# A two-layer graph network on one core: first weight chunks loaded and flipped by half columns, neighbour sums issued singly behind half products

## The chip, the cores and the metric

The kernel runs on one core of a Trainium2 chip. That core has a matrix engine (TensorE, "PE" in the profile), a vector engine (VectorE, "DVE"), a scalar engine (ScalarE, "ACT"), a general-purpose engine (GpSimd, "POOL") that here issues the indexed transfers, and SyncE ("SP"), which issues the plain ones. Each engine works through its own queue of instructions; a scheduler fixes the order of each queue when the kernel is built, and semaphores make one engine wait for another. The metric is the device time of one launch in microseconds (us), lower is better.

## What is computed

`x` has 2708 rows of 1024 numbers in fp32, and `adj` is a 0/1 matrix of 2708 x 2708 with few ones (the first rows have the most). The reference is

```python
# layer 0: attention over the neighbours of each row
q, k, v = x @ Wq.T + bq, x @ Wk.T + bk, x @ Wv.T + bv
z = (q @ k.T) / sqrt(1024) * adj
z = where(z == 0, -10000, z)
x = layernorm(x + relu(softmax(z, axis=1) @ v))
# layer 1: sum over the neighbours of each row
x = layernorm(x + adj @ (x @ W1) + b1)
```

Since `adj` is sparse, the kernel never forms the 2708 x 2708 scores. It reads `adj` once, makes of each row a list of its neighbours' numbers, and gathers the neighbours' rows. The scores come from one product `y = x M`, with M made of Wq and Wk ahead of everything else, and layer 1 is worked out as `(adj @ x) @ W1`. A dense version of the whole lies behind a test of the data and isn't executed here.

## The kernel before

**Tiles.** The rows are worked on in 22 blocks of 128 (block numbers 0 to 21). `SLOTS` says for each block how many neighbours its longest list has: 15 for block 0 down to 0 for blocks 20 and 21. Rows with very long lists, the hub, are dealt out over a block of parts of their own (`"hub"`, `HUB_SLOTS = 11`), whose partial sums in `part` are brought back by a matmul with the 0/1 matrices `to_h` and `to_0`.

**Products.** A product of two blocks with a 1024 x 1024 weight is made with seven half products instead of eight (`pair_products`, L335; `half_products`, L308): the weight's quarters w11, w12, w21, w22 are taken with three differences t2, t3, t4 (and t1, which overwrites w12), and the left side with four sums `s_all` of the turned blocks (L1212 to L1215). A half product is four matmuls of 128 x 128 by 128 x 512, which the profile shows as eight records at L311. Its result in PSUM is evicted by `add` (L333) or, in layer 1, by `whole` (L1517), both on DVE, with a priority that the scheduler puts ahead of other work. A block is turned ("flipped") by TensorE through PSUM, with ACT's copies of the result to SBUF: `flip` (L953, L954) takes one transpose for each 128 x 128 chunk, and `flip_shares` (L966) a matmul with a given matrix in place of the identity.

**The start.** SP's queue issues the loads in program order: the 8 chunks of WqT, then the 8 of WkT, each 512 KB (L142, L144), then pieces of `adj`. TensorE flips each chunk in two groups of four transposes as it lands (`flip_w`, L281), into one of three PSUM buffers (`p_tr`); the groups are copied out by ACT (L286) and DVE (L284) in turn. Meanwhile DVE forms Wq^T bk, one column of numbers from each chunk of Wq (`junkd`, L298), and POOL and ACT form Wk^T bq (L301, L302). The product of the two flipped weights, M, is the first work of `pair_products`, with its differences of weights made by DVE at L783 and L784.

**Between the layers.** When a block of layer 0 is done, it is normalised (`norm`, L998 to L1014; for the last block `norm_halves`, L1019 to L1032, on statistics by half rows at L1239) and scattered to `x_d` in device memory (L940, on POOL). Every gather of layer 1 reads `x_d`, so the first of them comes behind the last scatter. To keep TensorE busy across that, `WARM = 13` matmuls without use are put there (L1530). W1 is loaded by quarters at the end of layer 0 (L1447).

**Layer 1.** The blocks are worked on in ten units of two, in the order of `units` (L1456). For each block `sum_rows` (L1472 to L1484) issues one gather for each slot (`gather_slot`, L483, on POOL) into one of nine `g` tiles or, for slot 0 of an ordinary block, straight into the sum's tile `r`; then DVE adds it, with the slot's column of 0/1 flags in `valid` as a factor (L1480). Where slot 0 can be missing (blocks 0, 7, 18 and 19 and the hub), a pass of `tensor_scalar` masks it into `r` (L1477). Blocks 18 and 19 (`single`) have no other slot. `turn1` flips the sums of a unit; `gather_x1` (L467, L1490) gathers the block's own row onto a copy of the bias; `work1` makes the seven half products; `finish1` normalises and scatters to the output.

**What sets the order.** The instructions of one unit are written in the order finish of the unit before, flips of the unit after, sums of the third unit after, products (L1542 to L1563), and the hub's sums stand in unit 4. The sums of a block are written in one go, without a tie to TensorE except in unit 0, where `follow` ties the first of them behind the flipping of a unit. `between` is a table by which layer 0 hangs a function behind the half product of a given number; `half_products` calls it with its last matmul. In layer 1 of the kernel before it isn't used. The four differences of W1 (t1 to t4, L1537 to L1540) are written behind the first flips, and `follow(..., firsts[0], same=True)` holds t1 behind the first mask pass on DVE.

Of the kernel before, what the change touches and what calls it, by code (L numbers as in the profile page):

```python
# [9 lines left out]
F32 = mybir.dt.float32  # L10
# [11 lines left out]
P = 128  # L22
# [8 lines left out]
WARM = 13  # L31
# [53 lines left out]
def sparse_part(ctx, tc, x, xT, adj, wqT, wkT, wvT, bq, bk, bv, w1, b1, out):  # L85
# [28 lines left out]
    with es:  # L114
# [26 lines left out]
        for c in range(DC):  # L141
            nc.sync.dma_start(out=wq_i[c // 2][:, c % 2, :], in_=wqT[c * P:(c + 1) * P, :])  # L142
        for c in range(DC):
            nc.sync.dma_start(out=wk_i[:, c, :], in_=wkT[c * P:(c + 1) * P, :])  # L144
# [128 lines left out]
        def flip_w(dst, src):  # L273

            n = 0
            for c in range(DC):
                for g in range(DC // 4):
                    tr = p_tr.tile([P, 4, P], F32, name="tr")
                    for k in range(4):
                        o = g * 4 + k  # L280
                        put = nc.tensor.transpose(tr[:, k, :], src(c)[:, o * P:(o + 1) * P], ident)  # L281
                    to = dst(c, g)
                    if n % 2:
                        nc.vector.tensor_copy(to, tr)  # L284
                    else:
                        nc.scalar.copy(to, tr)  # L286
                    n += 1
            return put

# [3 lines left out]
        flip_w(lambda c, g: wq_of(c)[:, g * 4:g * 4 + 4, :], lambda c: wq_i[c // 2][:, c % 2, :])  # L293
        flipped = flip_w(lambda c, g: wk_o[g][c // 4][:, :, c % 4 * P:(c % 4 + 1) * P], lambda c: wk_i[:, c, :])
# [5 lines left out]
        for c in (*range(2, DC), 0, 1):  # L300
            nc.gpsimd.tensor_tensor(wk_i[:, c, :], wk_i[:, c, :], bq_bc, op=ALU.mult)  # L301
            put = nc.scalar.activation(junk[:, :D], wk_i[:, c, :], AF.Copy, accum_out=y_col[:, c:c + 1])  # L302
            follow(put, flipped)
# [1159 lines left out]
        firsts = []  # L1463

        def sum_rows(b, k=0, behind=None):
            if b == "hub":
                n, tab, ok, r = P, tab_h, valid_h, part
            else:
                n, tab, ok = (P, tab0, valid0) if b == 0 else (rows[b], tabs[:, b, :SLOTS[b]], valid[:, b, :SLOTS[b]])
                r = (cp if k else rp).tile([P, D], F32, name="r", bufs=3 if k else RB)  # L1470
            for j in range(tab.shape[1] if b else J0):
                if j == 0 and b not in [0, "hub"] + single + MIXED:  # L1472
                    gather_slot(x1_d[:, :], tab[:n, 0:1], n, r)
                    continue
                xg = gather_slot(x1_d[:, :], tab[:n, j:j + 1], n, g_tile())
                if j == 0:
                    put = nc.vector.tensor_scalar(r[:n], xg[:n], ok[:n, 0:1], None, op0=ALU.mult)  # L1477
                    firsts.append(put)
                else:
                    put = nc.vector.scalar_tensor_tensor(r[:n], xg[:n], ok[:n, j:j + 1], r[:n], op0=ALU.mult, op1=ALU.add)  # L1480
                if behind is not None:
                    follow(put, behind, same=True)
                    behind = None
            return r  # L1484
# [399 lines left out]
```

## Time and profile before

| | us |
|---|---|
| median of 3 runs | 1009.27 |
| lowest, highest | 1007.11, 1018.39 |
| profiled execution, its own time | 1011.19 |
| its span, first to last instruction | 1009.5 |
| TensorE busy, layer 1 from 725 to 996 us of the span | 257.7 of 271.0 |
| DVE busy, the same stretch | 186.6 |
| POOL busy, the same stretch | 178.2 |
| DVE busy, 30 to 60 us | 30.0 of 30.0 |

The profile's times count from the start of the span. L and a number is the line of the kernel. A line of a timeline gives the start, the duration of the instruction (or of a run of like ones, then with x and their number), the engine, line and operation, what it writes and reads, and in brackets the engine's idle time before it and what ended that. A line of the list of waits gives the waiting engine and line, what it waited for, then the total in us, the number of times and the longest. TensorE's granted clock averaged 0.983 of full speed over the span.

### The profile page before, as it was taken

How to read it: one execution, taken by the hardware profiler on the slowest of the kernel's cores; microseconds unless marked ns; L12 is line 12 of the kernel's file. 1: busy time of each engine (PE TensorE's matmuls, PEld its weight loads, DVE VectorE, ACT ScalarE, POOL GpSimd, SP SyncE). 2: the span in 40 equal slices, each digit the busy share in tenths (PEclk: the TensorE clock that was granted, in tenths of full speed). 3: DMA queues.
4: the chain of work that ended last, by engine and by line, in shares of the span. 5: the costliest groups of instructions: out<-in, count | busy, mean ns of one | idle time of the engine just before them, and what ended most of it. 6: DMA issues, size and time to landing. Idle time of an engine off the chain costs nothing.

```text
span 1009.5 us, 10470 instructions
## 1 busy us (share of the span) xinstructions
PE 957.8 (95%) x2723; PEld 452.3 (45%) x2723; DVE 815.7 (81%) x1813; ACT 461.5 (46%) x1142; POOL 553.2 (55%) x443
## 2 busy tenths in 40 slices
PE   7989999999999999999899999999899899999994
PEld 6434444444444444454444444444444444435441
DVE  8999996995678896998899999984668977868532
ACT  4553466655543434233643544563242444252832
POOL 3841056133677574445466785621877878868420
PEclk9999999999999999999999999999999999989998
DMA  8475687769889676346537897756887699977631
GB/s 346 152 238 177 209 262 223 232 229 249 237 250 326 219 231 211 118 141 194 167 97 227 266 304 236 220 170 228 199 285 226 210 319 338 300 234 199 213 105 45
DMA packets 101342, 222.92 MB, mean 221 GB/s; under 512 B 19492, under 2 KB 46892, under 8 KB 101272
## 3 DMA queue, kind: packets, MB, share of 16 engines
q0 software_dynamic: 49424, 152.74, 49.8%
q1 hardware_dynamic: 51848, 69.41, 21.2%
q8 instruction: 23, 0.38, 0.1%
q14 instruction: 47, 0.39, 0.1%
HBM read 211.80 MB, written 33.64 MB: 243 GB/s over the span
## 4 chain that ended last, share of the span: by engine, by line
PE 52%; DVE 20%; issue 11%; DMA 7%; POOL 4%; ACT 4%; SPq 0%; POOLq 0%; DVEq 0%; ACTq 0%
PE po L311 29%; PE po L391 11%; PE tr L391 5%; PE tr L311 3%; DVE r L1097 3%; DVE junkv L1038 2%; DMA xr<-x_d,tabs 2%; DVE t L333 2%; DVE r L1480 2%; POOL wk_i L301 1%; POOL g L483 1%; DVE junkv L1294 1%; DVE at_a L242 1%; PE tr L953 1%; DMA g<-x_d,tabs 1%
## 5 line engine op out<-in xcount | busy, mean ns | idle before, releaser
L483 POOL DMA_INDIRECT g<-in_x_dram,tabs x84 | 112.6, 1341 | 81.9 <-DVE past_end L663 26.9
L311 PE MATMUL po<-t,s_all 128*128 128x512 f32 x320 | 146.2, 599 | 7.5 <-issue 3.8
L391 PE MATMUL po<-m,xt 128*128 128x512 f32 x288 | 124.8, 592 | 0.0
L1480 DVE SCALAR_TENSOR_TENSOR r<-g,valid,r 128x1024 f32<-128x1024 f32 x77 | 98.0, 1280 | 11.9 <-DMA g<-x_d,tabs 7.2
L311 PEld LDWEIGHTS po<-t,s_all 128*128 128x128 f32 x320 | 60.5, 191 | 85.8 <-issue 77.0
L483 POOL DMA_INDIRECT g<-x_d,tabs x66 | 77.4, 1172 | 26.0 <-issue 13.7
L1097 DVE SCALAR_TENSOR_TENSOR r<-g,pr,r 128x1024 f32<-128x1024 f32 x64 | 81.9, 1281 | 6.4 <-ACT r L1095 5.8
L1038 DVE SCALAR_TENSOR_TENSOR junkv<-yg,g 128x1024 uint8<-128x1024 f32 x69 | 84.4, 1224 | 2.6 <-DMA g<-in_x_dram,tabs 2.0
L391 PEld LDWEIGHTS po<-m,xt 128*128 128x128 f32 x288 | 54.6, 190 | 68.2 <-issue 67.4
L954 ACT COPY rT<-tr 128x512 f32<-128x512 f32 x76 | 41.6, 587 | 95.1 <-PE tr L953 93.5
L1000 ACT ACTIVATE junks<-t,lnm 128x1024 uint8<-128x1024 f32 (+1 forms) x40 | 45.8, 1144 | 84.6 <-DVE lnm L998 84.5
L242 DVE FIND_INDEX8 at_a<-ones,a 128x8 uint16<-128x234 f32 (+5 forms) x132 | 82.2, 627 | 0.0
L311 PE MATMUL po<-w,rT 128*128 128x512 f32 x160 | 75.2, 612 | 4.4 <-DVE t L1517 4.2
L256 ACT ACTIVATE junk<-a 128x2756 uint8<-128x2756 uint32 (+1 forms) x22 | 55.0, 2501 | 42.8 <-issue 15.8
L311 PE MATMUL po<-t,rT 128*128 128x512 f32 x160 | 73.7, 603 | 0.4 <-DVE t L1517 0.4
L311 PE MATMUL po<-wv,rT 128*128 128x512 f32 x160 | 73.5, 604 | 0.0
L311 PE MATMUL po<-w,s_all 128*128 128x512 f32 x160 | 73.4, 598 | 0.0
L311 PE MATMUL po<-wv,s_all 128*128 128x512 f32 x160 | 72.3, 592 | 0.0
L462 ACT ACTIVATE junka<-xt 128x128 f32<-128x128 f32 x168 | 51.7, 308 | 37.9 <-PE po L311 18.3
L1038 DVE SCALAR_TENSOR_TENSOR junkv<-xr,g 128x1024 uint8<-128x1024 f32 x37 | 45.4, 1226 | 19.1 <-DMA g<-in_x_dram,tabs 11.3
L940 POOL DMA_INDIRECT x_d<-t,tabs x22 | 27.7, 1257 | 51.3 <-ACT t L1014 17.6
L391 PE MATMUL tr<-m,xt 128*128 128x512 f32 x128 | 55.6, 592 | 0.0
(423 smaller groups left out, 1835.7 us busy)
## 6 DMA issues: line engine op xcount, KB each, us to landing
xt<-in_xT_dram SPq DMA_DIRECT2D x21, 512.0 KB
y_d<-yo SPq DMA_DIRECT2D x21, 512.0 KB
a<-in_adj_dram SPq DMA_DIRECT2D x21, 413.0 KB
a<-in_adj_dram SPq DMA_DIRECT2D x21, 338.0 KB
a<-in_adj_dram SPq DMA_DIRECT2D x21, 263.0 KB
wq_i<-in_wqT_dram SPq DMA_DIRECT2D x8, 512.0 KB
wk_i<-in_wkT_dram SPq DMA_DIRECT2D x8, 512.0 KB
wv<-in_wvT_dram SPq DMA_DIRECT2D x16, 256.0 KB
```

The lines of the kernel that those rows point to most:

```text
L242: put = nc.vector.max_index(at[:n, i], ones[:n, :8], a[:n, cuts[i] + 8 * i:cuts[i + 1] + 8 * i + 8])
L256: put = nc.scalar.activation(junk[:n], loaded[b][:n, :AW].bitcast(U32), AF.Sign, accum_out=cnt[:n, b:b + 1])
L311: put = nc.tensor.matmul(acc, a[:, k], w[:, k], start=start and k == 0, stop=stop and k == DC // 2 - 1, skip_group_check=True)
L391: put = nc.tensor.matmul(po, xts[b][:, c, :], m_q[c // 4][h][:, c % 4], start=(c == 0), stop=(c == DC - 1))
L462: put = nc.scalar.activation(junka[:, :xt.shape[2]], xt[:, c, :], AF.Copy, accum_out=xs[:, c, b:b + 1])
L483: nc.gpsimd.indirect_dma_start(out=dst[:n], out_offset=None, in_=src, in_offset=bass.IndirectOffsetOnAxis(ap=at, axis=0), bounds_check=N - ...
L940: put = nc.gpsimd.indirect_dma_start(out=dst, out_offset=bass.IndirectOffsetOnAxis(ap=tabs[:n, b, ROW:ROW + 1], axis=0), in_=src[:n], in_o ...
L954: nc.scalar.copy(rT[:, g * 4:g * 4 + 4, :], tr)
L1000: nc.scalar.activation(junks[:n], t[:n], AF.Square, bias=nm[:n], accum_out=vs[:n])
L1038: put = nc.vector.scalar_tensor_tensor(junkv[:n], yg[:n], scale, xg[:n], op0=ALU.mult, op1=ALU.mult, accum_out=s)
L1097: nc.vector.scalar_tensor_tensor(r[:n], xg[j][:n], pr[:n, j:j + 1], r[:n], op0=ALU.mult, op1=ALU.add)
L1480: put = nc.vector.scalar_tensor_tensor(r[:n], xg[:n], ok[:n, j:j + 1], r[:n], op0=ALU.mult, op1=ALU.add)
```

## The change

The change has three parts. **First**, chunks 0 to 3 of both weights are loaded by half columns, the left halves of Wq's and Wk's four chunks ahead of the right halves, and then the chunks 4 to 7 whole. The flips follow that order. The order of the columns at L301 becomes 0 to 7. **Second**, the sums of layer 1 become single functions, one for each slot (`sums_of` and its `slot`). Those of units 0 and 1 are still written at the entry; all others are put behind half products through `between`: 0, 0, 0, 3, 3, 3 and 4 behind the seven of unit 0, and two behind each one after that, in the order units 2 to 6, hub, units 7 to 9. Each is tied to its half product's last matmul by `follow` with a semaphore, and the hub's and all units' sums are required to be placed when the loop ends. The tie of t1 is left out (the four differences are L1543 to L1546 in the changed kernel), and two more warming matmuls are added. **Third**, blocks 18 and 19 are gathered straight into a `g` tile, and no pass masks them; instead they are turned by `flip_shares` with a diagonal matrix of their flags, which two DVE operations build from the identity in the tiles `far_h` and `far_0`, free by then.

```diff
--- before.py
+++ after.py
@@ -28,7 +28,7 @@
 HUB_SLOTS = 11
 HUB_KEYS = 80
 RUN = 12
-WARM = 13
+WARM = 15
 FAMILY = 8
 
 
@@ -138,10 +138,12 @@
         nc.sync.dma_start(out=bk_sb, in_=bk)
         wq_i = [wm_pool.tile([P, 2, D], F32, name=f"wq_i{q}", tag=f"m{q}") for q in range(4)]
         wk_i = wk_pool.tile([P, DC, D], F32, name="wk_i")
-        for c in range(DC):
-            nc.sync.dma_start(out=wq_i[c // 2][:, c % 2, :], in_=wqT[c * P:(c + 1) * P, :])
-        for c in range(DC):
-            nc.sync.dma_start(out=wk_i[:, c, :], in_=wkT[c * P:(c + 1) * P, :])
+        first, second = range(DC // 2), range(DC // 2, DC)
+        loads = [(w, c, h) for h in range(NH) for w in "qk" for c in first] + [(w, c, None) for w in "qk" for c in second]
+        for w, c, h in loads:
+            cs = slice(0, D) if h is None else slice(h * HALF, (h + 1) * HALF)
+            nc.sync.dma_start(out=(wq_i[c // 2][:, c % 2] if w == "q" else wk_i[:, c])[:, cs],
+                              in_=(wqT if w == "q" else wkT)[c * P:(c + 1) * P, cs])
 
         nc.scalar.preload_act_table_set("natural_log_exp_and_others")
         ident = const.tile([P, P], F32, name="ident")
@@ -270,34 +272,28 @@
         wq_o = [wv_pool.tile([P, DC, 2 * P], F32, name=f"wq_o{q}", tag=f"v{q}") for q in range(4)]
         wk_o = [[wb.tile([P, DC // 2, HALF], F32, name=f"wk_o{g}{h}", bufs=1) for h in range(NH)] for g in range(DC // 4)]
 
-        def flip_w(dst, src):
-
-            n = 0
-            for c in range(DC):
-                for g in range(DC // 4):
-                    tr = p_tr.tile([P, 4, P], F32, name="tr")
-                    for k in range(4):
-                        o = g * 4 + k
-                        put = nc.tensor.transpose(tr[:, k, :], src(c)[:, o * P:(o + 1) * P], ident)
-                    to = dst(c, g)
-                    if n % 2:
-                        nc.vector.tensor_copy(to, tr)
-                    else:
-                        nc.scalar.copy(to, tr)
-                    n += 1
-            return put
-
         def wq_of(i):
             return wq_o[i // 2][:, :, i % 2 * P:(i % 2 + 1) * P]
 
-        flip_w(lambda c, g: wq_of(c)[:, g * 4:g * 4 + 4, :], lambda c: wq_i[c // 2][:, c % 2, :])
-        flipped = flip_w(lambda c, g: wk_o[g][c // 4][:, :, c % 4 * P:(c % 4 + 1) * P], lambda c: wk_i[:, c, :])
+        flips = [(w, c, g) for g in range(NH) for w in "qk" for c in first] + [
+            (w, c, g) for w in "qk" for c in second for g in range(NH)]
+        for n, (w, c, g) in enumerate(flips):
+            src = wq_i[c // 2][:, c % 2] if w == "q" else wk_i[:, c]
+            tr = p_tr.tile([P, 4, P], F32, name="tr")
+            for k in range(4):
+                o = g * 4 + k
+                flipped = nc.tensor.transpose(tr[:, k, :], src[:, o * P:(o + 1) * P], ident)
+            to = wq_of(c)[:, g * 4:g * 4 + 4, :] if w == "q" else wk_o[g][c // 4][:, :, c % 4 * P:(c % 4 + 1) * P]
+            if n % 2:
+                nc.vector.tensor_copy(to, tr)
+            else:
+                nc.scalar.copy(to, tr)
         load_adj()
         load_adj()
         for c in range(DC):
             nc.vector.scalar_tensor_tensor(junkd, wq_i[c // 2][:, c % 2, :], scale, bk_bc, op0=ALU.mult,
                                            op1=ALU.mult, accum_out=u_col[:, c:c + 1])
-        for c in (*range(2, DC), 0, 1):
+        for c in range(DC):
             nc.gpsimd.tensor_tensor(wk_i[:, c, :], wk_i[:, c, :], bq_bc, op=ALU.mult)
             put = nc.scalar.activation(junk[:, :D], wk_i[:, c, :], AF.Copy, accum_out=y_col[:, c:c + 1])
             follow(put, flipped)
@@ -1460,28 +1456,27 @@
         units = [(19, 18), (17, 16), (15, 1), (14, 2), (7, 8), (9, 3), (4, 10), (5, 11), (6, 0), (12, 13)]
         assert sorted(last + [b for unit in units for b in unit]) == list(range(NB))
         last_norm = applied[-1]
-        firsts = []
-
-        def sum_rows(b, k=0, behind=None):
+
+        def sums_of(b, k=0):
             if b == "hub":
                 n, tab, ok, r = P, tab_h, valid_h, part
             else:
                 n, tab, ok = (P, tab0, valid0) if b == 0 else (rows[b], tabs[:, b, :SLOTS[b]], valid[:, b, :SLOTS[b]])
-                r = (cp if k else rp).tile([P, D], F32, name="r", bufs=3 if k else RB)
-            for j in range(tab.shape[1] if b else J0):
-                if j == 0 and b not in [0, "hub"] + single + MIXED:
+                r = g_tile() if b in single else (cp if k else rp).tile([P, D], F32, name="r", bufs=3 if k else RB)
+
+            def slot(j, behind=None):
+                if j == 0 and b not in [0, "hub"] + MIXED:
                     gather_slot(x1_d[:, :], tab[:n, 0:1], n, r)
-                    continue
+                    return
                 xg = gather_slot(x1_d[:, :], tab[:n, j:j + 1], n, g_tile())
                 if j == 0:
                     put = nc.vector.tensor_scalar(r[:n], xg[:n], ok[:n, 0:1], None, op0=ALU.mult)
-                    firsts.append(put)
                 else:
                     put = nc.vector.scalar_tensor_tensor(r[:n], xg[:n], ok[:n, j:j + 1], r[:n], op0=ALU.mult, op1=ALU.add)
                 if behind is not None:
-                    follow(put, behind, same=True)
-                    behind = None
-            return r
+                    follow(put, behind)
+
+            return r, [lambda behind=None, j=j: slot(j, behind) for j in range(tab.shape[1] if b else J0)]
 
         def gather_x1(b, k=0):
 
@@ -1504,7 +1499,8 @@
             scatter(out, b, n, t, "out")
 
         def turn1(unit, rs):
-            return turn_pair([lambda rT, b=b, r=r: flip_shares([(part, to_h), (r, to_0)], rT) if b == 0 else flip(r, rT)
+            return turn_pair([lambda rT, b=b, r=r: flip_shares([(part, to_h), (r, to_0)], rT) if b == 0 else
+                              flip_shares([(r, only[b])], rT) if b in only else flip(r, rT)
                               for b, r in zip(unit, rs)], cp)
 
         def work1(unit, A, S, xrs):
@@ -1531,26 +1527,43 @@
             follow(put, products[-1], same=True)
 
         got1, turned1, pending = {}, {}, []
-        got1[0] = [sum_rows(b, k) for k, b in enumerate(units[0])]
-        got1[1] = [sum_rows(b, k) for k, b in enumerate(units[1])]
+
+        def begin_sums(u):
+            both = [sums_of(b, k) for k, b in enumerate(units[u])]
+            got1[u] = [r for r, _ in both]
+            return [slot for _, slots in both for slot in slots]
+
+        for b, to in zip(single, (far_h, far_0)):
+            nc.vector.tensor_scalar(to, ident, valid[:, b, 0:1], None, op0=ALU.mult)
+        only = dict(zip(single, (far_h, far_0)))
+        for u in range(2):
+            for slot in begin_sums(u):
+                slot()
         turned1[0] = turn1(units[0], got1.pop(0))
-        follow(nc.vector.tensor_sub(t1, t1, w11), firsts[0], same=True)
+        nc.vector.tensor_sub(t1, t1, w11)
         nc.vector.tensor_sub(t2, w22, t1)
         nc.vector.tensor_sub(t3, t2, w11)
         nc.vector.tensor_sub(t4, w21, t2)
         xrs = {0: [gather_x1(b, k) for k, b in enumerate(units[0])]}
+        to_sum, sums_left = list(range(2, 7)) + ["hub"] + list(range(7, len(units))), []
+
+        def some_sums(count, put):
+            for _ in range(count):
+                if not sums_left and to_sum:
+                    u = to_sum.pop(0)
+                    sums_left.extend(sums_of(u)[1] if u == "hub" else begin_sums(u))
+                if sums_left:
+                    sums_left.pop(0)(put)
+
         for i, unit in enumerate(units):
             for p in pending:
                 finish1(*p)
             if i + 1 < len(units):
                 turned1[i + 1] = turn1(units[i + 1], got1.pop(i + 1))
                 xrs[i + 1] = [gather_x1(b, k) for k, b in enumerate(units[i + 1])]
-            if i == 0:
-                got1[2] = [sum_rows(b, k, halves_turned[-1]) for k, b in enumerate(units[2])]
-            if i + 3 < len(units):
-                got1[i + 3] = [sum_rows(b, k) for k, b in enumerate(units[i + 3])]
-            if i == 4:
-                sum_rows("hub")
+            at = len(began)
+            for k, count in enumerate((0, 0, 0, 3, 3, 3, 4) if i == 0 else (2,) * 7):
+                between[at + 1 + k] = [lambda put, count=count: some_sums(count, put)]
             pending = list(zip(unit, *work1(unit, *turned1.pop(i), xrs.pop(i))))
             if i == len(units) - 4:
                 some = test_scores()
@@ -1559,6 +1572,7 @@
             if i in (4, 6):
                 b = last[i // 2 - 2]
                 pending.append((b, gather_x1(b), None))
+        assert not to_sum and not sums_left
         for p in pending:
             finish1(*p)
         raised = nc.values_load(flag, min_val=0, max_val=1, skip_runtime_bounds_check_because="a comparison's result")
```

## The prediction

> **What bounds the kernel now.** I read the page's totals first, then the waits of TensorE, then its timeline at the two places that the change touches.
>
> ```profile
> PE 957.8 (95%) x2723; PEld 452.3 (45%) x2723; DVE 815.7 (81%) x1813; ACT 461.5 (46%) x1142; POOL 553.2 (55%) x443
> ```
>
> TensorE is busy 957.8 of 1009.5 us, so it is the bound, and 51.7 us of idle time (1009.5 − 957.8) plus what it loses at a low clock is all that a reordering can win. Its list of waits says what ended that idle time (total, times, longest):
>
> ```profile
> PE po L311 <- DVE t L1517: 4.6, 2, 4.2
> PE tr L311 <- DVE m L333: 4.3, 1, 4.3
> PE po L311 <- issue: 3.8, 2, 2.0
> ...
> PE tr L953 <- DVE r L1477: 2.6, 1, 2.6
> ...
> PE tr L966 <- DVE r L1480: 2.0, 1, 2.0
> ```
>
> Four of the five lie in layer 1 or at its entry, and all name VectorE (DVE); the second is the start. In TensorE's timeline, the start and the hub's sums:
>
> ```profile
> 54.36 5.21 PE L311 MATMUL tr<-wk_o,wq_o 128*128 128x512 f32 x8 [4.33 <-DVE m L333]
> ...
> 885.58 2.07 PE L311 MATMUL po<-w,rT 128*128 128x512 f32 x2 [4.16 <-DVE t L1517]
> 887.45 5.01 PE L311 MATMUL po<-t,rT 128*128 128x512 f32 x8
> ```
>
> A half product is 8 records at 0.43 us, 3.43 us; after both waits it takes over 5. Each long wait is paid again in clock. Last, the entry to layer 1, in the timelines of DVE and of TensorE:
>
> ```profile
> 699.63 0.21 DVE L1019 BATCH_NORM_AGGREGATE mv<-halves 128x2 f32<-128x12 f32 x1
> ...
> 710.26 0.75 DVE L1477 TENSOR_SCALAR r<-g,valid 128x1024 f32<-128x1024 f32 x1 [8.45 <-DMA g<-x_d,tabs]
> 710.93 2.28 DVE L1537 TENSOR_TENSOR w<-w,w 128x2048 f32<-128x2048 f32 x1
> ```
>
> ```profile
> 697.24 11.32 PE L1530 MATMUL tr<-y_bc,ident 128*128 128x512 f32 x26
> 711.16 1.07 PE L953 MATMUL tr<-ident,r 128*128 128x128 f32 x8 [2.60 <-DVE r L1477]
> 712.46 3.50 PE L311 MATMUL po<-w,rT 128*128 128x512 f32 x4 [0.24 <-ACT rT L954]
> ```
>
> The last layernorm (699.63) leads through a scatter (702.56) and a gather (706.12) to the first mask pass (710.26) and the first flip (711.16); the four weight differences stand behind that pass. This chain has no slack.
>
> **What the Trainium skill says.** "TensorE: Matmul & The Clock Gate", Part 1 (The HAM clock gate): an idle window of about 3.4 us halves the clock, and as long of sustained work restores it. The trace agrees: 4 records took 3.50 us at 712.46 where 4 × 0.43 = 1.72 is usual; here even the 2.60 us before the flips was enough. Same page, "Architectural detail": DVE's queue is strictly first in, first out. The trace shows it: the eviction of L1517 at 884.84 runs behind two sums of L1480 (882.32, 2.60 us). "SBUF — State Buffer", Who interferes with whom: a DVE operation with two SBUF inputs contends with a GpSimd (POOL) one that reads SBUF. Here the same L298 takes 1.22 us alone and 2.17 us beside POOL's L301, and the gather issues beside the weight differences take 2.5 to 3.1 us instead of 1.0.
>
> **Part 1, half columns.** Removed: nothing; 8 loads of 512 KB become 16 of 256 KB. The same 8 MB arrive at the same pace (about 1.33 us per 512 KB), so the flips should only come in another order: both left halves first, so that the products of 512 columns could start before the rest is there. But the L298 pass over chunk 0 stands in DVE's queue ahead of the flip copies (the instruction order of the changed kernel shows it third from there) and reads both halves. Its second half is now the 9th load of half a chunk; four and a half chunks have then arrived. The flips of the fourth chunk started at 10.30 before, so half a chunk more (0.66 us) makes it usable at about 10.96, instead of 6.85. Everything in DVE's queue is moved by 4.1 us, TensorE's flips too, since their three PSUM buffers wait for DVE's copies. Against this, DVE's idle gaps between 8 and 27 us (1.3 us) are absorbed, and nearly two more of the eight L298 passes fall beside POOL's L301 (+0.95 each, 1.9 in sum): 4.1 − 1.3 + 1.9 = +4.7 us at the last flip copy. The weight differences L783 and L784 follow (3.90 and 4.20 us), then the evictions of the first products, on which the wait of 54.36 hangs. Fewer column searches stand ahead of these evictions than before, about 2 us of them. So +4.7 − 2 = **+2.7 us**. The bound below is −4 (TensorE gets 5 or 6 half products into the flips, 17 us of work, and the 4.33 us wait with its 1.6 us of cold clock could go), the one above +4.7 (nothing is absorbed). From 60 us on the order is the same, and m_t2 is ready 12 us ahead of its use: the shift neither grows nor is caught up.
>
> **Part 2a, the entry.** The tie that held the first weight difference behind the first mask pass is gone, and so is that pass. In the changed order the four differences (L1543 to L1546) stand in DVE's queue ahead of the last aggregation: the second ahead of the last L333 eviction, the third and fourth behind the two statistics. W1's last quarter lands at 695.5 and is usable at about 696.9. Chain from there: second difference 696.9 to 699.2; eviction, first statistic and residual pass (3 × 0.69) to 701.3; third difference 2.28, second statistic 0.69, fourth difference 2.28; aggregation at 706.6 instead of 699.63: **+7.0 us** on the last scatter and the first gather. Off it goes the mask pass (0.75 and its 0.14 of hand-over, **−0.9**): the first flip at 711.16 + 7.0 − 0.9 = 717.3. The two added warming matmuls end at 697.24 + 11.32 + 2 × 2 × 0.435 ≈ 710.3, seven us early, so TensorE is cold, as it is before. The flips of blocks 19 and 18 are now 2 records a chunk instead of 1 (0.11 us each warm; 8 chunks × 2 blocks × 0.11 = 1.8 us, up to 3.5 cold). In return POOL's gathers no longer meet the differences: two issues of 2.6 us become 1.0, −3.2 on POOL, of which I take 2.5 on the path, since the first S1·t2 at 725.04 waits for the last of these gathers. Net there: 7.0 − 0.9 + 1.8 to 3.5 − 2.5 = +5.4 to +7.1; I take **+6.7**. Below, with W1's quarter landing earlier, 1.0 us less (DVE is free for the second difference at 695.9), +4.4; above, +9.6, if nothing of POOL's 2.5 counts.
>
> **Part 2b, the sums.** From 725.04 to the last matmul at 995.83 are 270.8 us. Without waits and at full clock the same records take 5 × 3.43 (rest of unit 0) + 9 × 24.05 (seven half products each) + 15 flips × 0.89 + 3.5 (block 0) + 0.4 = 250.9. So **19.9 us** are waits and cold clock: 0.96 + 2.04 + 1.44 + 1.74 + 0.42 + 0.87 + 4.16 + 2.03 + 0.25 = 13.9 of waits (at 725, 750, 765, 788, 797, 804, 881, 923, 954), and about 6 of clock after them (2.8 after 881, 2 after 923). Most are evictions or half products behind a bunch of sums. The change puts at most two sums behind each half product: 2 × 1.28 + the eviction 0.69 = 3.25 of 3.43 us. This fits, but s_all's four sums (0.69 each) and the layernorm's small steps come on top. Of a unit's 14 slots some two are plain gathers without a sum, so DVE has about 12 × 1.28 + 7 evictions and 4 sums of s_all × 0.69 = 22.9 us and 1 of small steps, of the 25.8 that a unit without stalls takes (827.61 to 853.42). What is late next: a gather that lands after its sum's turn holds up the eviction behind it, and block 0 with its 13 gathers, now issued behind the out scatters, must be ready by the unit's flip. I leave R = 4.5 us of the 19.9 (two of the old waits, 0.96 and about 2, and 1.5 of clock); from 0 to 11, the latter if only the hub's wait with its clock (7.0) and two of the small ones go. Gain **15.4**. Sum: +2.7 + 6.7 − 15.4 = **−6.0**.
>
> **The sum against its own run.** The profiled execution took 1011.19 us (span 1009.5, 1.7 around it); so 1005.2 for such a one. It lies 0.2% above the median of 1009.27; the same 6.0 below the median is **1003.3**.
>
> **Rivals.** *The entry and the start cost nothing* (B): the differences find DVE waiting for PSUM anyway and L298 runs in a gap. For it: DVE is idle 2.74 us before 690.58, 1.76 before 694.01. Against: the aggregation stands behind all four. Then start 0, entry +1.5, R = 3: 1.5 − 16.9 = −15.4, **993.9 us**. *Half the stalls stay* (D): the waits are those of single late gathers, not of bunches; for it, the 2.04 at 750 came with DVE waiting 3.56 us for a gather. R = 10: +9.4 − 9.9, **1008.8**. *DVE becomes the bound* (C), slower: sums behind half products wait at DVE's head for gathers, with the evictions queued behind them. POOL is busy 178 of these 271 us and the DMA share is 0.96 between 800 and 880. Two such waits of 1.1 us in each of ten units make R = 22: +9.4 + 2.1 = +11.5, **1020.8**; it decides for slower from R = 10.5 us, about 1 us a unit.
>
> **How the numbers follow.** The forecast has 0.50, B 0.20, D 0.20, C 0.10. Measurements of this kernel tell 1% (10 us) from no change at best. Faster by over 1% (under 999.2): all of B and the quarter of the forecast with R near 0 and a start of −4: 0.20 + 0.13 = 0.33. Slower (over 1019.4): 0.08 of C. Within: the rest, 0.59. The range leaves out the lower half of B and C: 994 to 1014.
>
> **What would show it.** Start: first L294 pass of DVE near 11 us instead of 6.85, and the wait before the product of 54.36 ending near 57. Entry: the four differences ahead of the aggregation, that near 706 and the first flip near 717. Layer 1: no idle stretch of TensorE above 1 us where the hub and block 0 are summed, and from the first S1·t2 to the last matmul about 255 us instead of 270.8. I am wrong if the aggregation stays near 700 (B), or if waits for L1513 recur unit by unit (C).

## The result, and the profile after

The changed kernel takes 1022.81 us in the median of 20 runs (1019.03 to 1028.53), the kernel before 1011.86 us (20 runs, 1006.71 to 1018.39). The ratio is 1.0118, with a 95% interval of 1.0099 to 1.0137: the change costs 1.2%, where the forecast had 0.6% less. (The ratios of this document were worked out apart from the medians, whose quotient is 1.0108 here; differences of that size are not to be read.) The profiled execution's span is 1020.3 us, beside 1009.5 before.

The page's totals of the changed kernel, then TensorE's list of waits (total, times, longest):

```profile
PE 962.4 (94%) x2743; PEld 460.1 (45%) x2743; DVE 807.5 (79%) x1813; ACT 465.9 (46%) x1142; POOL 548.4 (54%) x443
```

```profile
PE tr L949 <- DVE r L1475: 12.8, 4, 4.8
PE tr L962 <- DMA g<-x_d,tabs: 6.9, 1, 6.9
PE po L307 <- DVE yo L329: 4.9, 2, 3.3
...
PE po L307 <- DVE r L1475: 2.1, 1, 2.1
```

The waits put down to evictions (before: L311 for L1517) are gone from layer 1's part of the list. In their place flips of neighbour sums (L949) wait for the last sum itself (L1475), 12.8 us in four pieces; the last line, one half product's 2.1 us, is looked at below. The second line is the entry, the third lies in layer 0. TensorE's timeline shows these waits, and that the longest are paid again in clock:

```profile
695.69 13.04 PE L1526 MATMUL tr<-y_bc,ident 128*128 128x512 f32 x30
715.64 3.75 PE L962 MATMUL tr<-far,g 128*128 128x128 f32 x16 [6.91 <-DMA g<-x_d,tabs]
...
763.05 1.06 PE L949 MATMUL tr<-ident,r 128*128 128x128 f32 x8 [2.83 <-DVE r L1475]
...
824.82 5.40 PE L307 MATMUL po<-w,s_all 128*128 128x512 f32 x8 [2.06 <-DVE r L1475]
...
865.10 1.94 PE L949 MATMUL tr<-ident,r 128*128 128x128 f32 x8 [4.79 <-DVE r L1475]
866.83 8.71 PE L307 MATMUL po<-w,rT 128*128 128x512 f32 x16
```

Eight transposes take 1.94 us after the wait instead of 1.04, and the next two half products 8.71 instead of 7.03. The half product of 824.82 hung on an eviction, as DVE's timeline just before it shows:

```profile
822.88 1.28 DVE L1475 SCALAR_TENSOR_TENSOR r<-g,valid,r 128x1024 f32<-128x1024 f32 x1 [6.25 <-DMA g<-x_d,tabs]
824.08 0.68 DVE L329 TENSOR_TENSOR xr<-po,xr 128x512 f32<-128x512 f32 x1
```

A sum waited 6.25 us for its gather, the eviction came behind it in DVE's queue and ended at 824.76, and the product began at 824.82.

Taking the same points of TensorE's timeline in both traces says where the time came from (warm: start of the warming matmuls, which is the end of layer 0's products; S1: the first product of unit 0 with `s_all`):

| us | before | changed | difference |
|---|---|---|---|
| first product with m_t2 | 59.41 | 60.28 | +0.9 |
| from there to warm | 637.8 | 635.4 | −2.4 |
| warm to S1, the entry | 27.8 | 34.3 | +6.5 |
| S1 to the end of the last matmul, layer 1 | 270.8 | 276.9 | +6.1 |
| sum | | | +11.1 |

The −2.4 lie in layer 0, where the change adds two small operations and, at its very end (690.32), the first weight difference. Its waits differ by some us in both directions; after one that is 2.5 us in both, for example, the two next records took 1.94 us in the one trace (497.57 before) and 1.12 in the other (498.98). The same stretch takes 634.6 to 640.1 us over all fourteen traces of this document, so the −2.4 is not told here as an effect. The last stretch has such a spread too: four traces with the sums at these places (the changed kernel, e1, e2 and e4 below) take 273.7 to 276.9 us, so the +6.1 could as well have been +3.

The entry, in DVE's timeline of the changed kernel:

```profile
695.92 2.29 DVE L1544 TENSOR_TENSOR t<-w,w 128x2048 f32<-128x2048 f32 x1
...
699.92 2.29 DVE L1545 TENSOR_TENSOR t<-t,w 128x2048 f32<-128x2048 f32 x1
702.12 0.69 DVE L1235 BATCH_NORM_STATS2 halves<-t 128x6 f32<-128x512 f32 x1
702.73 2.28 DVE L1546 TENSOR_TENSOR t<-w,t 128x2048 f32<-128x2048 f32 x1
704.92 0.20 DVE L1015 BATCH_NORM_AGGREGATE mv<-halves 128x2 f32<-128x12 f32 x1
```

The aggregation comes 9.2 us after warm (704.92 − 695.69); before it was 2.4 (699.63 − 697.24). And layer 1, around the longest wait, in DVE's and then in POOL's timeline:

```profile
852.61 0.69 DVE L1513 SCALAR_TENSOR_TENSOR t<-po,xr 128x512 f32<-128x512 f32 x1 [2.74 <-PE po L307]
...
858.73 2.61 DVE L1475 SCALAR_TENSOR_TENSOR r<-g,valid,r 128x1024 f32<-128x1024 f32 x2 [5.42 <-issue]
...
863.67 1.28 DVE L1475 SCALAR_TENSOR_TENSOR r<-g,valid,r 128x1024 f32<-128x1024 f32 x1
```

```profile
835.13 0.99 POOL L479 DMA_INDIRECT g<-x_d,tabs  x1 [0.30 <-issue]
841.26 2.02 POOL L936 DMA_INDIRECT out_dram<-t,tabs  x1 [5.14 <-ACT t L1010]
843.59 2.08 POOL L463 DMA_INDIRECT xr<-x_d,tabs  x1 [0.31 <-issue]
845.98 1.57 POOL L463 DMA_INDIRECT xr<-x_d,tabs  x1 [0.30 <-issue]
847.86 1.02 POOL L936 DMA_INDIRECT out_dram<-t,tabs  x1 [0.30 <-issue]
849.18 1.02 POOL L479 DMA_INDIRECT r<-x_d,tabs  x1 [0.30 <-PE po L307]
```

The flip at 865.10 waits for the sum of 863.67, the last of its block, which has only just been made. DVE stood idle for 5.42 us ahead of its last three sums. POOL had issued the gathers for them only from 849.18 on, behind a scatter to the output that waited 5.14 us for ScalarE's normalisation and behind gathers of own rows (`xr`). The DMA engines had little to do meanwhile (mean busy share 0.29 from 841 to 845) and were full afterwards (1.01 from 849 to 858.7, where the first of the three sums starts). So two readings are open: the sums and their gathers come too late in the order (theory 1), or their tie to a half product holds DVE's queue (theory 2). Both leave the same idle time in this trace.

### The profile page after: what moved, and what is told of

The parts are those of the page before. It is cut to its first block, busy times and chain, and to the rows that moved or that the text cites. A ratio compares the mean times of both kernels' runs of the same rounds, so it can differ in the third digit from the quotient of the medians.

```text
span 1020.3 us, 10507 instructions
## 1 busy us (share of the span) xinstructions
PE 962.4 (94%) x2743; PEld 460.1 (45%) x2743; DVE 807.5 (79%) x1813; ACT 465.9 (46%) x1142; POOL 548.4 (54%) x443
## 4 chain that ended last, share of the span: by engine, by line
PE 56%; DVE 16%; DMA 10%; issue 9%; POOL 6%; ACT 2%; SPq 0%; POOLq 0%; DVEq 0%; ACTq 0%
PE po L307 33%; PE po L387 11%; PE tr L387 5%; PE tr L307 3%; DMA g<-x_d,tabs 3%; POOL wk_i L297 2%; DVE r L1475 2%; DVE r L1093 2%; DMA wk_i<-in_wkT_dram 2%; PE tr L949 2%; DVE junkv L1034 1%; POOL g L479 1%; DVE t L329 1%; DMA g<-in_x_dram,tabs 1%; PE po L438 1%
## 5 line engine op out<-in xcount | busy, mean ns | idle before, releaser
L1475 DVE SCALAR_TENSOR_TENSOR r<-g,valid,r 128x1024 f32<-128x1024 f32 x77 | 98.5, 1282 | 41.0 <-DMA g<-x_d,tabs 33.7
L479 POOL DMA_INDIRECT g<-x_d,tabs x66 | 74.9, 1135 | 22.4 <-issue 17.4
L307 PE MATMUL po<-w,s_all 128*128 128x512 f32 x160 | 75.7, 613 | 2.1 <-DVE r L1475 2.1
L1485 ACT COPY xr<-bias 128x1024 f32<-128x1024 f32 (+1 forms) x22 | 22.8, 1046 | 87.3 <-DVE t L1513 85.3
```

The costliest lines, as they stand in the source:

```text
L307: put = nc.tensor.matmul(acc, a[:, k], w[:, k], start=start and k == 0, stop=stop and k == DC // 2 - 1, skip_group_check=True)
L479: nc.gpsimd.indirect_dma_start(out=dst[:n], out_offset=None, in_=src, in_offset=bass.IndirectOffsetOnAxis(ap=at, axis=0), bounds_check=N - ...
```

## The experiments

Each ratio is to runs of the kernel before on the same chip in the same group. The median of those was 1011.2 us in the first group of four, then 1008.9, 1007.8 and 1011.3, so times of different groups are compared only through their ratios, and 0.2% between groups is not a difference.

**e1, the start as before.** The loads, the flips and the order of the columns of the kernel before are put back:

```diff
-        loads = [(w, c, h) for h in range(NH) for w in "qk" for c in first] + [(w, c, None) for w in "qk" for c in second]
...
+        for c in range(DC):
+            nc.sync.dma_start(out=wq_i[c // 2][:, c % 2, :], in_=wqT[c * P:(c + 1) * P, :])
```

> The changed kernel with the loads, the flips and the column order of the start as in the kernel before; the rest stays changed. The two traces put the start at +0.9 us (first product with m_t2 at 60.28 instead of 59.41), my forecast had +2.7. If the traces are right, 1021 to 1023 us beside 1022.8; if the forecast's step is right, about 1020. No theory of layer 1 expects anything of it.

Measured: 1022.6 us, ratio 1.0124 (1.0083 to 1.0165), against 1.0118 with the change. The first part costs or gains nothing that these runs can tell. The traces agree: the ten with the new start reach the first product with m_t2 at 59.2 to 60.5 us, the four with the old start at 59.4 to 61.0, so the +0.9 of the table is within the spread of executions. In the profile of the changed kernel the queue of DVE did stop as forecast, even longer; here DVE's timeline, then TensorE's:

```profile
12.26 1.23 DVE L294 SCALAR_TENSOR_TENSOR junkd<-wq_i,a 128x1024 uint8<-128x1024 f32 x1 [7.85 <-DMA wq_i<-in_wqT_dram]
```

```profile
46.16 14.29 PE L307 MATMUL tr<-wk_o,wq_o 128*128 128x512 f32 x32
60.28 2.31 PE L307 MATMUL po<-m_t,s_b 128*128 128x512 f32 x5
```

The pass over the first chunk starts at 12.26 instead of 6.85, and the flips end at 36.9 instead of 27.7. The eviction on which the wait of 54.36 hung comes at 56.02 instead of 53.64, 2.4 us later. But TensorE starts its products so late that it still has some to make then: it runs through to 60.28 without a stop. The wait of 4.33 us, which all four traces with the old start have, is gone, and with it the cold clock behind it (5.21 us for 8 records instead of 3.60, 1.6 us): 2.4 − 1.6 is about the 0.9 between these two traces.

**e2, the differences behind the last layernorm.** `normed` holds the last DVE operation of `norm_halves`:

```diff
-        nc.vector.tensor_sub(t1, t1, w11)
+        follow(nc.vector.tensor_sub(t1, t1, w11), normed[-1], same=True)
```

> The changed kernel with the first of the four weight differences tied behind the last operation of the last layernorm on DVE, so that all four run in DVE's idle time ahead of the first gather. If they were on the path to the last scatter, the aggregation comes back by 6 to 7 us against the end of layer 0's products and the time is 1016 to 1018 us. If DVE had idle time for them, or layer 1 gives the gain back in its waits for sums, it stays at 1021 to 1024.

Measured: 1016.55 us, ratio 1.0053 (1.0029 to 1.0077). The aggregation is back at 2.4 us after warm (702.62 − 700.23), and the entry takes 30.0 us instead of 34.3. So the order of the differences was on the path to the last scatter. Layer 1 keeps its waits for sums (10.9 us at L949).

**e3, the sums one unit sooner.**

```diff
-        to_sum, sums_left = list(range(2, 7)) + ["hub"] + list(range(7, len(units))), []
+        to_sum, sums_left = list(range(3, 7)) + ["hub"] + list(range(7, len(units))), []
...
+            if i == 0:
+                for n, slot in enumerate(begin_sums(2)):
+                    slot(halves_turned[-1] if n == 0 else None)
```

> The changed kernel with the sums of the third unit written in one go ahead of unit 0's products, as in the kernel before, and the single sums behind half products from the fourth unit on: every later sum and its gather comes about one unit sooner. Theory 1 (the sums are ready too late: their gathers stand behind the unit's out scatters and end just when the flip wants them): the five waits of flips for L1475 go, 13 us with about 7 us of cold clock after them, 1003 to 1010 us. Theory 2 (it is the tie of each sum to its half product that holds DVE's queue): little changes, 1019 to 1025 us.

Measured: 1011.37 us, ratio 0.9995 (0.9979 to 1.0011), so 1.2% less than the changed kernel. Layer 1 takes 265.9 us instead of 276.9. TensorE's list of waits of this run:

```profile
PE tr L962 <- DMA g<-x_d,tabs: 8.2, 1, 8.2
...
PE po L307 <- DVE xr L329: 5.5, 3, 3.5
...
PE tr L949 <- DVE r L1475: 3.1, 2, 2.7
```

The waits of flips for sums fell from 12.8 to 3.1 us with nothing but a place in the order changed. What came up instead are 5.5 us of half products that wait for evictions into `xr`: 3.5 of it for an eviction that waited for its gather of own rows, the rest for evictions behind sums that waited for theirs.

**e4, the sums without the tie.**

```diff
-                    sums_left.pop(0)(put)
+                    sums_left.pop(0)()
```

> The changed kernel with the single sums written at the same places, but without the semaphore that ties each to its half product; the order on each engine is the same but for a few instructions of units 0 and 1. Theory 2 (the tie): DVE can take a sum as soon as its gather is there, the waits of the flips go, 1005 to 1012 us. Theory 1 (too late in the queues): the gathers come no sooner, 1019 to 1025 us.

Measured: 1021.55 us, ratio 1.0093 (1.0057 to 1.0129), which includes the changed kernel's 1.0118; TensorE still waits 10.9 us at L949 for L1475. Theory 2 is refuted as the main cause: without the semaphore DVE waits no less for gathers of sums (40 us from 735 us on, 28 in the changed kernel).

**e5, both edits together** (e2 and e3).

> The changed kernel with both edits of the runs before: the four differences behind the last layernorm and the sums one unit sooner. The one gave 6.3 us, the other 11.4 us. If they are two separate costs they add up: 1004 to 1007 us. If the late sums hid part of the entry's cost, less than 14 us in all: 1008 to 1011.

Measured: 1007.04 us, ratio 0.9985 (0.9969 to 1.0001). By ratio it is 1.3% below the changed kernel, where the two edits alone sum to 1.9%. In the trace the parts do stand side by side: entry 31.1, layer 1 266.6 us. How far they add up is not settled, since e5 stands in another group than e2 and e3. Both together undo the loss and leave the spreading with a gain that these runs can hardly tell from nothing.

**e6, two units written ahead**:

```diff
-        to_sum, sums_left = list(range(3, 7)) + ["hub"] + list(range(7, len(units))), []
+        to_sum, sums_left = list(range(4, 7)) + ["hub"] + list(range(7, len(units))), []
...
-            for k, count in enumerate((0, 0, 0, 3, 3, 3, 4) if i == 0 else (2,) * 7):
+            for k, count in enumerate((0,) * 7 if i == 0 else (2,) * 7):
```

The sums of the third and fourth unit are written in one go ahead of unit 0's products.

> As the run beside it, but the sums of the third and fourth unit are written in one go and the single ones begin with the fifth unit behind unit 1, which is the lead of the kernel before; only the spreading is left of the change to the sums. If lead is what counts, up to the point where it is enough, the waits for L1475 are gone and it takes 1002 to 1006 us. If a longer lead only moves gathers onto the transfers of the own rows (waits of evictions for xr), it is no better than the run beside it, within 3 us.

Measured: 1005.83 us, ratio 0.9963 (0.9947 to 0.9980), layer 1 in 265.2 us. The time is in the first expected span (by the ratio, 0.9963 of 1011.2, it is above it), but only 1.2 us (0.2%) below e5, so it does not tell the two expectations apart. It couldn't well: from the fifth unit on its sums have the same places as e5's, give or take a few, and only the fourth unit's come sooner. The hub's first sum starts 117.3 us after S1 in e6, 115.5 in e5 and 136.1 in the changed kernel. So this is no test of a longer lead, and e3 and e5 already have the lead that its expectation calls the one of the kernel before: the sums of the third unit after the current one in each iteration. Of the 8.7 us that are still waited in layer 1, 6.0 are half products that wait for `xr`, and 2.0 a flip that waits for a sum.

**e7, the kernel before with its bunches one unit later.**

```diff
-            if i + 3 < len(units):
-                got1[i + 3] = [sum_rows(b, k) for k, b in enumerate(units[i + 3])]
-            if i == 4:
+            if i and i + 2 < len(units):
+                got1[i + 2] = [sum_rows(b, k) for k, b in enumerate(units[i + 2])]
+            if i == 5:
                 sum_rows("hub")
```

> The kernel before with its sums in bunches, as they were, but written one unit later (the sums of the second unit after the current one instead of the third; the hub's in the sixth unit instead of the fifth). If lead is the cause whatever the form of the sums, it loses about what the changed kernel lost in layer 1: 8 to 16 us, 1019 to 1027. If only single sums tied to half products need the lead, it stays at 1008 to 1014.

Measured: 1020.0 us, ratio 1.0097 (1.0066 to 1.0129). The kernel before loses by this alone about what the whole change lost; layer 1 takes 279.3 us. So the lead counts also for sums in bunches. TensorE's list seems to name other waits:

```profile
PE tr L953 <- ACT nmr L1013: 7.3, 4, 2.9
PE po L311 <- DVE xr L333: 7.3, 4, 2.9
PE tr L953 <- DVE r L1480: 4.5, 1, 4.5
```

Only 4.5 us are named after a sum; four flips are put down to ScalarE's small steps of the layernorm. But a flip reads only `r` and the identity, and the timelines of TensorE and DVE show each of the four starting just after a sum has ended, the first for example:

```profile
779.62 1.52 PE L953 MATMUL tr<-ident,r 128*128 128x128 f32 x8 [2.45 <-ACT nmr L1013]
```

```profile
778.20 1.28 DVE L1480 SCALAR_TENSOR_TENSOR r<-g,valid,r 128x1024 f32<-128x1024 f32 x1
```

The sum ends at 779.48, 0.14 us before the flip; in the changed kernel the flip of 865.10 follows its sum (863.67 + 1.28) by 0.15. Counted in this way, flips wait for sums 12.7 us in e7's layer 1, 12.0 to 13.8 in the four traces with the changed kernel's places, 4.3 in the kernel before, 1.0 in e11 and 2.0 to 4.4 in the runs that give the lead back (e3, e5, e6, e8, e10, e12).

**e8, the mask pass again**: e5 with the sums of blocks 18 and 19 masked into `r` and transposed; the two diagonal matrices aren't built.

```diff
-                r = g_tile() if b in single else (cp if k else rp).tile([P, D], F32, name="r", bufs=3 if k else RB)
+                r = (cp if k else rp).tile([P, D], F32, name="r", bufs=3 if k else RB)
...
-                if j == 0 and b not in [0, "hub"] + MIXED:
+                if j == 0 and b not in [0, "hub"] + single + MIXED:
...
-                              flip_shares([(r, only[b])], rT) if b in only else flip(r, rT)
+                              flip(r, rT)
```

> As the first run of these four, but blocks 18 and 19 are masked by a pass on DVE and turned by transposes again, as in the kernel before. My forecast priced the third part at the entry as: the pass and its hand-over 0.9 us, the added flip records 1.8 to 3.5 us. So this should be 1 to 2.6 us faster at the first S1 product than the run beside it; if the pass is dearer than that, because it stands behind other work on DVE, it is slower.

Measured: 1003.69 us, ratio 0.9933 (0.9904 to 0.9961), beside 0.9985 for e5 in the same group: 3.4 us faster. The sign is as expected; the trace shows only 0.7 us of it at the entry (30.4 instead of 31.1), the rest is spread over stages that this edit doesn't touch. And e10, which is the same edit on e6, has 0.9957 beside e6's 0.9963, with an entry of 31.2 us beside 29.9. So whether the third part cost anything is not settled.

**e9, each gather six slots ahead of its sum**, the sums as in the changed kernel: `slot` is split into a `fetch` with the gather and the sum.

```diff
+                for fetch, _ in sums_left[fetched[0]:6 + 1]:
+                    fetch()
...
-                    sums_left.pop(0)(put)
+                    sums_left.pop(0)[1](put)
```

> The changed kernel with each gather issued six slots ahead of its sum, the sums where the change put them. If the sums are late because their gathers stand too far back in POOL's queue, behind scatters that wait for ScalarE, DVE's waits for gathers (33.7 us at L1475) and TensorE's for sums (13.4 us) mostly go: 1005 to 1013 us. If the sums themselves come too late behind their half products, gathers that are there sooner don't help: 1018 to 1024.

Measured: 1015.54 us, ratio 1.0082 (1.0050 to 1.0115), so its interval overlaps that of the changed kernel. In time it lies between the two expectations, but the kernel before took less time in this group too (1007.8); by the ratio it is in the second. In the trace DVE waits 13 us for gathers of sums from 735 us on, instead of 28, and the flips still wait 9.6 us for sums (counted as in e7), instead of 13.4. Layer 1 takes 272.6 us, little below the 273.7 to 276.9 of the four traces with these places. So the place of the gathers in POOL's queue is at most a part of the lateness, and gathers that come sooner don't replace sums that come sooner, as in e3.

**e10, all three mended**: e6 and e8 together.

> The changed kernel with the differences behind the last layernorm, the single sums with the lead of the kernel before (from the fifth unit on), and the mask pass with transposes for blocks 18 and 19. The longer lead gave 0.2% and the mask pass 0.5% beside the same kernel, so 1000 to 1003 us where the kernel before takes 1009, 0.7 to 0.9% faster. If both gains are the same idle time, no better than the mask pass alone, 0.993 of before.

Measured: 1003.96 us, ratio 0.9957 (0.9944 to 0.9971). That is faster than the kernel before, but short of the 0.7 to 0.9% that was expected, and no better than e8. Layer 1 takes 261.4 us in its trace, the shortest of all, and the entry 31.2.

**e11, the kernel before with the differences early**, tied behind the last layernorm as in e2.

> The kernel before with only one edit: the first weight difference tied behind the last operation of the last layernorm instead of behind the first mask pass, so that all four are done before the first gather arrives. The gather issues that took 2.5 to 3.1 us beside the differences should take 1.0, and the first S1 product start up to 3 us sooner: 1006 to 1008 us where the kernel before takes 1009. If that product waits for something else that comes no sooner, no change within 1 us.

Measured: 1009.38 us, ratio 1.0020 (1.0003 to 1.0037): not faster. The entry takes 30.8 us instead of 27.8. The gathers that came later are quick now, but the last scatter and the first gathers have become slow; POOL's timeline of e11, and of the kernel before:

```profile
700.12 2.28 POOL L940 DMA_INDIRECT x_d<-t,tabs  x1 [4.62 <-ACT t L1031]
705.01 2.11 POOL L483 DMA_INDIRECT g<-x_d,tabs  x1 [2.62 <-DMA x_d<-t,tabs]
707.43 1.87 POOL L483 DMA_INDIRECT g<-x_d,tabs  x1 [0.30 <-issue]
```

```profile
702.56 0.95 POOL L940 DMA_INDIRECT x_d<-t,tabs  x1 [4.62 <-ACT t L1031]
706.12 1.03 POOL L483 DMA_INDIRECT g<-x_d,tabs  x1 [2.60 <-DMA x_d<-t,tabs]
707.45 1.00 POOL L483 DMA_INDIRECT g<-x_d,tabs  x1 [0.30 <-issue]
```

DVE's timeline has the differences at 699.28 to 708.4, beside just these. DVE's idle time ahead of the first gather isn't free for a long operation with two inputs in SBUF: POOL is on the path there.

**e12, e10 with the tie behind the first mask pass**, as in the kernel before.

```diff
-        follow(nc.vector.tensor_sub(t1, t1, w11), normed[-1], same=True)
+        follow(nc.vector.tensor_sub(t1, t1, w11), firsts[0], same=True)
```

> The kernel with all three points mended (0.9957 of before), but with the first weight difference tied behind the first mask pass, as in the kernel before, instead of behind the last layernorm. In the runs with the tie behind the layernorm the last scatter took 2.28 us on POOL instead of 0.95 and the first two gathers 2.1 and 1.9 instead of 1.0, beside the differences; from the end of layer 0's products to the first S1 product they need 30 to 31 us, the kernel before 27.8. If that contention on the path is the cause, the stretch comes back to 28 us and the time is 0.2 to 0.4% shorter: 0.992 to 0.994 of before. If the differences cost the same wherever they meet POOL's work, no change, 0.995 to 0.997.

Measured: 1007.7 us, ratio 0.9967 (0.9949 to 0.9985), no better than e10. The cause was right and the gain didn't come. The last scatter takes 0.95 us again, and the entry is down to 26.6 us from 31.2. But layer 1 takes 268.7 instead of 261.4: the differences now meet the gathers of the own rows (one issue 3.15 us), and a half product waits for an eviction into `xr` that stands behind a sum whose gather was late (2.81 us at 737). Of the 7.3 us more, 4.2 lie ahead of the flip of 756 (754.76 in e10). That the contention is paid in either place fits this, but e5 and e6, with the other tie, have such a wait at about 735 too (1.63 and 3.02 us), so it is not shown.

## Why the prediction was wrong

It forecast 1003.3 us (994 to 1014) and gave slower by over 1% a chance of 0.08; measured were 1022.8, 8.8 above its range. Point by point:

- **Part 2a, the entry: right.** +6.7 us forecast at S1, +6.5 measured from warm (34.3 to 35.7 us in the five traces with this entry, 27.8 and 27.0 in the two with the old one). The mechanism is the one named, four differences ahead of the aggregation: +7.0 forecast, +6.8 measured after warm. e2 shows it by undoing it. Its deduction for POOL's gathers holds in the trace of the changed kernel (0.99 us per issue instead of 2.6). What e11 and e12 add is that this saving comes only from where the differences meet POOL, and that it costs elsewhere.
- **Part 1, the start: the first steps right, the size not.** +2.7 forecast, +0.9 between the two traces, nothing measurable in e1 or over the fourteen traces. The first pass came later still (12.26 instead of 11). The last flip copy ended 10.5 us later (39.53 instead of 29.07), not 4.7, and the weight differences began 8.2 later. Of this, 5.8 us and not 2 were absorbed ahead of the eviction, so that its +2.4 is near the forecast by luck. The term that was left out is the clock: without the wait there is no cold half product behind it, −1.6 us. It stood in the lower bound alone, together with the wait. And few products went in between the flips (10 records, 4 before), not the 5 or 6 half products of that bound.
- **Part 2b, the sums: wrong, and this decided.** R was put at 4.5 us of the 19.9, at most 11; it is 276.9 − 250.9 = 26.0 (22.8 to 24.5 in the three other traces with these places), of which 15.4 are waits and the rest mostly clock after them. The step that failed is "What is late next". It checked that two sums and an eviction fit into the time of a half product (3.25 of 3.43 us), that is the rate, and asked of one block only whether it would be ready by the flip. It didn't ask when the last sum of each unit is due. Before, the sums of the third unit after the current one are written in iteration i; behind half products, two a time, the sums of a unit fill about one unit's fourteen places and end in the unit ahead of the one in which they are flipped. The old order had a unit more of lead. e3 restores one unit and gains 1.2%; e7 takes one from the kernel before and loses 1.0%, with flips that wait for sums as here; e4 excludes the tie as the main cause. What the lead hides is less sure: the trace shows gathers held up in POOL's queue by scatters, but e9 moves the gathers ahead and gains little.
- **Rival C** came near the time (1020.8) with R = 22, and was right that single sums wait for gathers at DVE's head (33.7 us at L1475, 13 times, 12.95 of it at the entry). The eviction behind such a sum was what TensorE waited for once in layer 1, at 824.82 (2.06 us and 1.8 of clock), just as C says, and two, one and four times in e1, e2 and e4 (1.7, 2.9 and 6.1 us); 13.4 of the 15.4 us were flips that waited for the sums, which C did not name. Its waits unit by unit were not there.
- **Part 3** was priced at +0.9 to +2.6 net. e8 agrees in sign, e10 beside e6 shows nothing; it stays open.

What the spreading is worth with enough lead is read from e10 beside e11, of one group and with the same entry: 1003.96 and 1009.38 us, layer 1 in 261.4 and 267.0. They differ in the spreading, and besides in the start and two warming matmuls, which e1 and the idle time ahead of the first flip leave without a measurable part. That is some 5.5 us, a third of the 15.4 forecast. e12 beside the kernel before, again with the same entry, gives less: 1007.7 and 1011.3 us, layer 1 in 268.7 and 270.8. New waits take the place of the old ones, in e10 3.7 us of flips for sums and 3.1 of half products for evictions into `xr`.

## What to carry to other kernels

When work is spread out behind other work, check two things: that it fits the rate, and by how much earlier than its use the last piece of each group ends, in the worst queue it goes through. A lead that looks like slack may be what keeps the last piece in time; here one unit of it was worth 1.0 to 1.2%. When a list of waits names an odd engine, look at what ended just before the wait did. And a vector engine's idle time is not free for an operation that slows another engine on the path.

## What was not expected of the hardware

The issue of an indirect scatter or gather on POOL took 0.95 to 1.03 us alone and 1.9 to 2.3 us (up to 3.1 in the kernel before) when a DVE operation with two fp32 inputs of 128x2048 in SBUF ran beside it (e2, e8, e11), so the long issues seen in the profile of before follow the differences wherever they are put. In the pages of the Trainium skill, "SBUF — State Buffer" ("Who interferes with whom") has such a DVE operation contend with a GpSimd instruction that reads SBUF. The same section infers that it leaves GpSimd's making of DMA descriptors alone; here an issue took about twice as long, and the measurement decides.

TensorE's clock fell after waits shorter than the idle window of about 3.4 us that "TensorE: Matmul & The Clock Gate" of the Trainium skill gives (Part 1): after 2.06 us at 824.82 the next half product took 5.40 us instead of 3.60, at a granted clock of 0.67. A half product of the same size took 3.70 after a wait of 2.04 us in the kernel before (752.26). So waits of 2 us are sometimes paid nearly double, and two executions can differ by it, as the example from layer 0 above shows.
